# The eleventh gate and up tiles of a gated FFN as one seven-product block product, and two PSUM banks that change places

## The chip, the cores and the metric

The kernel runs on one core of a Trainium2 chip, in float32 throughout. The metric is the device time of one execution in microseconds; before the change its median over three runs is 2418.64 us (2414.57 to 2418.65). One more execution was taken with the hardware profiler; the profile, and every duration quoted here, is of that execution.

The engines are named as in the profile: PE is the matrix engine's matmuls and PEld its weight loads, DVE the vector engine, ACT the activation engine, POOL the GpSimd engine, and SP the engine whose queue issues nearly all transfers. A letter q behind an engine is its instruction queue (SPq).

## The reference, cut to what matters

The input x has 64 sequences of 128 tokens of 512 features. A normalised copy of x goes through a linear cross attention over a context, whose gated result is added to x; then the feed-forward part (FFN) works on a second normalised copy, here `x1n`:

```python
g = x1n @ gate_w.T * gate_s          # 512 -> 1408
u = x1n @ up_w.T   * up_s            # 512 -> 1408
hdn = silu(g) * u
out = x + tanh(g_ffn) * (hdn @ down_w.T * down_s)   # 1408 -> 512
```

The 1408 hidden units are eleven tiles of 128. The weights are given as inputs, so anything made from them is made once and used for all tokens.

## The kernel before, in words

**Groups.** The 64 sequences are worked in 16 groups of four, `g` from 0 to 15; a group is 512 tokens. Pass 1 (to about 430 us) normalises x and sums the scores over all sequences; between its groups the generator `prepare_weights` makes the weight combinations of the later pass. Pass 2 runs for each group the attention of group g interleaved with the FFN of group g - 1; the last FFN runs alone. `interleave` takes steps from the generators in proportion to given step counts (`FFN_STEPS` for the FFN), so that each `yield` in `ffn` is a place where attention work may be put. The program written so is then put in order, for each engine, by the framework's list scheduler, which may move an instruction ahead of others that don't depend on it. Each engine works its own list from front to back.

**Seven products in place of eight.** A product of two matrices, each seen as 2 by 2 blocks, needs eight block products if it is done plainly. `combine_a` makes four sums of one side's blocks (called GS1 to GS4 here) and `combine_b` four of the other's, and seven products of these, with a few additions of the results, give the same output. The kernel does this for tile pairs of gate and up: with the tiles j and 5 + j (`NJ` is 5) of both matrices, and for `x1nT` (features on partitions, 512 tokens) split into two halves of the features and two halves of the tokens (`HT`, 256 tokens). `combine_tokens` makes the four token sums `t` once for each group, on POOL.

In `ffn`, one j runs through the seven products GA11, GS1, GA12, GS2, GS3, GS4, GA22. Their results meet in PSUM: `bank_a` collects GA11 and GA12, `bank_f` holds GS1, and `bank_c` (one of the two halves of `banks_c`, which `next_c` gives in turn) starts from a copy of GA11 that ACT makes and collects GS2, GS3 and GA22; `bank_b` starts from a copy of `bank_c` after GS2 and collects GS4. GS1's result is copied to `m5` in SBUF. So between the products lie ACT copies, and DVE additions (`c22`, `c12`), and each of these must be done before the next product may write the bank that it read. `hidden` does silu on ACT and the multiplication on DVE. In these products the gate and the up tile of a j are two halves of one bank (`product`, two halves of 256 columns).

**The eleventh tile.** Eleven tiles make five pairs and one tile over (`REST` is 10). Its gate and up columns are worked plainly after the five j: `gu_rest[:, s]`, loaded in `constants`, against all of `x1nT`, four matmuls of 512 columns for gate into `bank_a` and four for up into `bank_f`; then one silu and one multiplication make `hrest`.

**Down.** The hidden result goes through seven products as well (`down_product`, DB11, DT1, DB21, DT2, DT3, DB22, DT4), five matmuls for each of two halves, with weights that `down` loads one product at a time; `down_rest` adds the eleventh tile's part, and `add` (DVE) adds the bank to x in SBUF. DB11 and DB21 use `bank_a`, DT1 and the first rest of the second pair `bank_f`, and the others `banks_c` and `bank_b`.

**The order of the transfers.** SP issues them in program order as the scheduler put them, each when its buffer is free: `gate_up(j + 1)` two transfers for each j, `down(m)` one for each product, between them the attention's.

A float32 matmul of the program is two matmul records on the chip, as the counts show: the eleventh tile's gate is 4 matmuls in each of 16 groups, and the profile has 128 records of it.

Of the kernel before, what the change touches and what calls it, by code (L numbers as in the profile page):

```python
# [8 lines left out]
F32 = mybir.dt.float32  # L9
AF = mybir.ActivationFunctionType  # L10
ALU = mybir.AluOpType
# [12 lines left out]
GA11, GS1, GA12, GS2, GS3, GS4, GA22 = range(7)  # L24
DB11, DB21, DB22, DT1, DT2, DT3, DT4 = range(7)
# [15 lines left out]
def flamingo_gated_layer(  # L41
# [21 lines left out]
    nc = tc.nc  # L63
    P = 128
# [3 lines left out]
    NC = DIM // P  # L68
    NI = INTER // P
    GB = 4  # L70
    NG = B // GB
    TOK = GB * S
    HT = TOK // 2
    HN = DIM // 2
    KC = NC // 2
    NJ = NI // 2
    REST = 2 * NJ
    assert S == P and H == NC and TOK == 512 and DIM == 512 and NI == REST + 1

    const = ctx.enter_context(tc.tile_pool(name="const", bufs=1))  # L80
# [36 lines left out]
    beta_sb = const.tile([P, NC], F32, name="beta_sb")  # L117
    gs_sb = const.tile([P, NI], F32, name="gs_sb")
    us_sb = const.tile([P, NI], F32, name="us_sb")
    gu_rest = const.tile([P, 2, NC, P], F32, name="gu_rest")  # L120
    dn_rest = const.tile([P, DIM], F32, name="dn_rest")


# [7 lines left out]
    bank_a = ps_bank.tile([P, TOK], F32, name="bank_a")  # L131
    bank_f = ps_bank.tile([P, TOK], F32, name="bank_f")
    bank_b = ps_bank.tile([P, TOK], F32, name="bank_b")
# [56 lines left out]
    def combine_a(engine, s, a11, a12, a21, a22):  # L190
        engine.tensor_tensor(s[0], a21, a22, ALU.add)  # L191
        engine.tensor_tensor(s[1], s[0], a11, ALU.subtract)
        engine.tensor_tensor(s[2], a11, a21, ALU.subtract)
        engine.tensor_tensor(s[3], a12, s[1], ALU.subtract)
# [40 lines left out]
    def constants():  # L235

        nc.sync.dma_start(out=gamma_sb, in_=gamma.rearrange("(c p) -> p c", p=P))
        nc.sync.dma_start(out=beta_sb, in_=beta.rearrange("(c p) -> p c", p=P))
        nc.sync.dma_start(out=gs_sb, in_=gate_s)
        nc.sync.dma_start(out=us_sb, in_=up_s)  # L240
        cols = slice(REST * P, INTER)
        for s, w in enumerate((gateT, upT)):
            nc.sync.dma_start(
                out=gu_rest[:, s], in_=w[:, cols].rearrange("(c p) i -> p c i", p=P)
            )

    def prepare_weights():

        constants()
        ds = once.tile([P, DIM], F32, name="ds")  # L250
        nc.sync.dma_start(out=ds, in_=down_s.partition_broadcast(P))
        nc.vector.tensor_scalar_mul(ds, ds, tanh_g[:, 1:2])
        yield


        raw = once.tile([P, NC, DIM], F32, tag="prep", name="wo_raw")
        nc.sync.dma_start(out=raw, in_=wo.rearrange("(c p) e -> p c e", p=P))
        nc.vector.tensor_scalar_mul(raw, raw, tanh_g[:, 0:1])
        t = once.tile([P, 4, KC, HN], F32, tag="prep2", name="wo_t")
        b = (  # L260
            raw[:, 0:KC, 0:HN], raw[:, 0:KC, HN:DIM], raw[:, KC:NC, 0:HN], raw[:, KC:NC, HN:DIM],
        )
        combine_b(nc.gpsimd, [t[:, i] for i in range(4)], *b)
        for m, src in ((DB11, b[0]), (DB21, b[2]), (DB22, b[3])):
            nc.sync.dma_start(out=wo_scr[m], in_=src)
        for i, m in enumerate((DT1, DT2, DT3, DT4)):
            nc.sync.dma_start(out=wo_scr[m], in_=t[:, i])
        yield


        for j in range(NJ + 1):
            i1, i2 = (j, NJ + j) if j < NJ else (REST, None)
            raw = once.tile([P, 2, DIM], F32, tag="prep", name="dn_raw")
            for q, i in enumerate((i1, i2)):
                if i is None:
                    nc.sync.dma_start(out=raw[:, q], in_=downT[i1 * P : (i1 + 1) * P])
                    nc.gpsimd.tensor_tensor(dn_rest, raw[:, q], ds, ALU.mult)
                    continue
                if j == NJ:
                    continue  # L280
                nc.sync.dma_start(out=raw[:, q], in_=downT[i * P : (i + 1) * P])
                nc.gpsimd.tensor_tensor(raw[:, q], raw[:, q], ds, ALU.mult)
            if j == NJ:
                yield
                continue
            t = once.tile([P, 4, HN], F32, tag="prep2", name="dn_t")
            b = (raw[:, 0, 0:HN], raw[:, 0, HN:DIM], raw[:, 1, 0:HN], raw[:, 1, HN:DIM])
            combine_b(nc.gpsimd, [t[:, i] for i in range(4)], *b)
            for m, src in ((DB11, b[0]), (DB21, b[2]), (DB22, b[3])):
                nc.sync.dma_start(out=dn_scr[m, :, j], in_=src)  # L290
            for i, m in enumerate((DT1, DT2, DT3, DT4)):
                nc.sync.dma_start(out=dn_scr[m, :, j], in_=t[:, i])
            yield

        for j in range(NJ):
            w = once.tile([P, 8, 2, KC, P], F32, tag="prep", name="gu_raw")
            i1 = slice(j * P, (j + 1) * P)
            i2 = slice((NJ + j) * P, (NJ + j + 1) * P)
            k1, k2 = slice(0, HN), slice(HN, DIM)
            for s, mat in enumerate((gateT, upT)):  # L300
                for m, k, i in ((GA11, k1, i1), (7, k1, i2), (GA22, k2, i2), (GA12, k2, i1)):
                    nc.sync.dma_start(
                        out=w[:, m, s], in_=mat[k, i].rearrange("(c p) i -> p c i", p=P)
                    )
            combine_a(
                nc.gpsimd, [w[:, m] for m in (GS1, GS2, GS3, GS4)],
                w[:, GA11], w[:, GA12], w[:, 7], w[:, GA22],
            )
            nc.sync.dma_start(out=gu_scr[0][j], in_=w[:, 0:3])
            nc.sync.dma_start(out=gu_scr[1][j], in_=w[:, 3:7])  # L310
            yield

    acc = banks_c[:, 1, :].rearrange("p (h s) -> p h s", h=H)

# [230 lines left out]
    def next_c():  # L545
        turn[0] ^= 1
        return banks_c[:, turn[0], :]
# [22 lines left out]
    def ffn(g, x_t, x1nT, tokens):  # L570
# [20 lines left out]
        for j in range(NJ):  # L591
# [34 lines left out]
                h11[:, j, :], h21[:, j, :], h12, h22[:, j, :],  # L626
            )
            yield
        for s, bank in enumerate((bank_a, bank_f)):
            for c in range(NC):  # L630
                nc.tensor.matmul(  # L631
                    bank, lhsT=gu_rest[:, s, c, :], rhs=x1nT[:, c, :],
                    start=(c == 0), stop=(c == NC - 1),
                )
            yield
        sil = work.tile([P, TOK], F32, tag="c", name="sil")
        nc.scalar.activation(sil, bank_a, AF.Silu, scale=gs_sb[:, REST:NI])
        nc.vector.scalar_tensor_tensor(
            hrest, bank_f, us_sb[:, REST:NI], sil, ALU.mult, ALU.mult
        )  # L640
        if g + 1 < NG:
            gu_next[0] = gate_up(0)

        def down_product(bank, m, lhs, start):
            dn = down(m)
            for i in range(2):
                for j in range(NJ):
                    nc.tensor.matmul(  # L648
                        bank[:, i * HN : (i + 1) * HN],
                        lhsT=lhs[:, j, i * P : (i + 1) * P],  # L650
                        rhs=dn[:, j, :],
                        start=(start and i == 0 and j == 0),
                        stop=(i == 1 and j == NJ - 1),
                        skip_group_check=True,
                    )
                yield

        def down_rest(bank, q, cols):
            for i in range(2):
                nc.tensor.matmul(  # L660
                    bank[:, i * HN : (i + 1) * HN],
                    lhsT=hrest[:, (2 * q + i) * P : (2 * q + i + 1) * P],
                    rhs=dn_rest[:, cols],
                    start=False, stop=(i == 1), skip_group_check=True,
                )

        def add(q, cols, bank):
            dst = x_t[q][:, :, cols]
            nc.vector.tensor_add(dst, dst, bank.rearrange("p (b d) -> p b d", b=2))

        d1, d2 = slice(0, HN), slice(HN, DIM)
        bank_c = next_c()
        yield from down_product(bank_a, DB11, h11, True)
        nc.scalar.copy(bank_c, bank_a)
        yield from down_product(bank_f, DT1, hs[:, 0], True)
        add(0, d2, bank_f)
        yield from down_product(bank_a, DB21, h21, False)
        down_rest(bank_a, 0, d1)
        add(0, d1, bank_a)
        yield  # L680
        yield from down_product(bank_c, DT2, hs[:, 1], False)
        nc.scalar.copy(bank_b, bank_c)  # L682
        down_rest(bank_f, 1, d2)
        add(1, d2, bank_f)
        yield
        yield from down_product(bank_c, DT3, hs[:, 2], False)
        add(1, d2, bank_c)
# [9 lines left out]
            nc.sync.dma_start(out=out[b : b + 2].rearrange("b s d -> s b d"), in_=x_t[q])  # L697

    gu_next = [gate_up(0)]
    FFN_STEPS = 1 + 7 * NJ + 2 + 17  # L700
    pending = (0, x_t, x1nT, combine_tokens(x1nT))
    x_next = load_x(1)
    c_next = [load_ctx(GB + j) for j in range(GB)]
# [71 lines left out]
```

## Time and profile before

| What | Value |
|---|---|
| median of three runs | 2418.64 us (2414.57 to 2418.65) |
| the profiled execution: its own time | 2416.87 us |
| its span, first to last instruction | 2415.1 us |
| PE busy | 2351.8 us, 97% of the span, 11480 matmul records |
| PEld busy | 1996.3 us, 83% |
| DVE, ACT, POOL busy | 802.0, 587.2, 686.2 us (33%, 24%, 28%) |
| the 16 DMA engines, mean busy share of the main queue | 49.1% |
| granted clock of the matrix engine, mean | 0.994 |
| one group of pass 2, from one start of the eleventh tile to the next (1384.4 to 1509.8 us) | 125.4 us |

How to read it: PE's busy time is the union of its records, so idle time is what is left. Of the 63 us in which PE did nothing, most lies before 507 us: the stretch from 0 to 507 us has PE busy 461.91 us. From there on a group of 125.40 us has PE busy 124.44 us. The waits of an engine are listed by the instruction that waited and the one that released it. The duration of a matmul record is longer than the distance to the next, since matmuls overlap; what counts is the distance from start to start.

### The profile page before, as it was taken

Reading aid. Unit: us, or ns where it says so; the run is one execution under the profiler, and the core shown is the slowest. Engines: PE = TensorE matmul, PEld = TensorE weight load, DVE = VectorE, ACT = ScalarE, POOL = GpSimd, SP = SyncE. Lnnn points to the kernel's source line nnn. Section 1 sums busy time; section 2 is a strip of 40 time slices with the busy share of each in tenths; the row PEclk is TensorE's granted clock in tenths of the full one; section 3 lists DMA queues with packets and bytes.
Section 4 is the critical chain, followed back from the end, with each engine's and each line's share of the span. In section 5 each row is a group of like instructions: output and inputs, shape, how many; then the busy total and the mean of one; then the engine's idle time right before and its main releaser. Section 6 shows DMA issues by size and latency. Waiting matters only on the chain.

```text
span 2415.1 us, 28827 instructions
## 1 busy us (share of the span) xinstructions
PE 2351.8 (97%) x11480; PEld 1996.3 (83%) x11480; DVE 802.0 (33%) x1541; ACT 587.2 (24%) x1076; POOL 686.2 (28%) x770
## 2 busy tenths in 40 slices
PE   7899998999999999999999999999999999999999
PEld 6777787888888888888888888888888888888887
DVE  6455433232323232323232323232323233232321
ACT  2232332312122222222221313131313131312121
POOL 3433003332323232323241414141414132232320
PEclk9999999999999999999999999999999999999999
DMA  7777544545454545444545444454545454544342
GB/s 262 243 251 251 172 144 131 214 131 185 139 173 150 176 143 173 146 166 148 168 157 165 164 146 162 159 168 140 175 145 165 140 178 133 182 133 149 118 147 72
DMA packets 136262, 396.31 MB, mean 164 GB/s; under 512 B 14272, under 2 KB 33856, under 8 KB 125248
## 3 DMA queue, kind: packets, MB, share of 16 engines
q1 hardware_dynamic: 132464, 392.63, 49.1%
q10 hardware_dynamic: 3664, 1.84, 0.3%
q8 instruction: 91, 1.49, 0.3%
q14 instruction: 43, 0.35, 0.0%
HBM read 345.26 MB, written 49.15 MB: 163 GB/s over the span
## 4 chain that ended last, share of the span: by engine, by line
PE 85%; DVE 5%; POOL 4%; DMA 3%; issue 1%; ACT 1%; SPq 0%; ACTq 0%; POOLq 0%; DVEq 0%
PE banks_c L169 17%; PE bank_a L169 12%; PE banks_c L648 9%; PE bank_b L169 6%; PE bank_a L648 6%; PE bank_f L169 4%; PE by L478 3%; PE bank_b L648 3%; PE bank_f L648 3%; PE pv L428 2%; PE bank_f L631 2%; PE bank_a L631 2%; PE bz L478 2%; PE bx L478 2%; PE banks_c L348 2%; PE po L438 2%
## 5 line engine op out<-in xcount | busy, mean ns | idle before, releaser
L169 PE MATMUL banks_c<-tcomb,gu 128*128 128x256 f32 x1920 | 453.9, 379 | 0.0
L169 PEld LDWEIGHTS banks_c<-tcomb,gu 128*128 128x128 f32 x1920 | 358.9, 190 | 46.3 <-ACT bank_b L604 0.7
L169 PE MATMUL bank_a<-x1nT,gu 128*128 128x256 f32 x1280 | 305.2, 381 | 6.8 <-ACT banks_c L596 6.7
L169 PEld LDWEIGHTS bank_a<-x1nT,gu 128*128 128x128 f32 x1280 | 237.6, 191 | 41.5 <-ACT banks_c L596 12.4
L146 POOL TENSOR_TENSOR rs<-ve,mhalf 128x1 f32<-128x1 f32 x128 | 72.5, 575 | 608.0 <-DVE ve L145 606.1
L191 POOL TENSOR_TENSOR hs<-h,h 128x256 f32<-128x256 f32 x80 | 58.0, 725 | 517.0 <-DVE h L584 517.0
L583 ACT ACTIVATE sil<-c,gs_sb 128x256 f32<-128x256 f32 x160 | 81.3, 508 | 345.1 <-DVE c L613 237.2
L169 PE MATMUL bank_b<-x1nT,gu 128*128 128x256 f32 x640 | 151.2, 379 | 0.0
L169 PE MATMUL bank_f<-tcomb,gu 128*128 128x256 f32 x640 | 151.2, 379 | 0.0
L613 DVE TENSOR_TENSOR c<-banks_c,m 128x512 f32<-128x512 f32 x80 | 55.3, 691 | 279.7 <-PE banks_c L169 279.7
L648 PE MATMUL banks_c<-dn_w,hs 128*128 128x256 f32 x640 | 146.0, 379 | 0.0
L648 PE MATMUL bank_a<-dn_w,h 128*128 128x256 f32 x640 | 143.5, 379 | 0.0
L648 PEld LDWEIGHTS bank_a<-dn_w,h 128*128 128x128 f32 x640 | 120.3, 190 | 16.3 <-issue 0.7
L169 PEld LDWEIGHTS bank_f<-tcomb,gu 128*128 128x128 f32 x640 | 120.5, 190 | 15.8
L169 PEld LDWEIGHTS bank_b<-x1nT,gu 128*128 128x128 f32 x640 | 120.5, 190 | 15.8
L648 PEld LDWEIGHTS banks_c<-dn_w,hs 128*128 128x128 f32 x640 | 119.2, 190 | 15.2 <-ACT bank_b L682 0.3
L596 ACT COPY banks_c<-bank_a 128x512 f32<-128x512 f32 x80 | 45.6, 570 | 301.6 <-PE bank_a L169 242.9
L584 DVE SCALAR_TENSOR_TENSOR h<-c,us_sb,sil 128x256 f32<-128x256 f32 x160 | 89.5, 559 | 83.8 <-ACT sil L583 83.8
L465 POOL TENSOR_TENSOR yT<-w_t,yT 128x512 f32<-128x512 f32 x64 | 81.1, 1268 | 121.3 <-ACT yT L460 121.3
L150 DVE BATCH_NORM_STATS2 st<-x_t 128x6 f32<-128x512 f32 x128 | 82.4, 683 | 82.2 <-DMA x_t<-in_x_dram 81.1
L584 DVE SCALAR_TENSOR_TENSOR h<-bank_a,us_sb,sil 128x256 f32<-128x256 f32 x80 | 38.6, 482 | 209.1 <-ACT sil L583 209.1
L188 POOL TENSOR_TENSOR tcomb<-x1nT 128x512 f32<-128x512 f32 x32 | 39.9, 1267 | 205.6 <-ACT x1nT L528 205.6
(134 smaller groups left out, 3651.9 us busy)
## 6 DMA issues: line engine op xcount, KB each, us to landing
gu<-gu_scr SPq DMA_DIRECT2D x80, 1024.0 KB, 4.9
dn_w<-dn_scr SPq DMA_DIRECT2D x112, 640.0 KB, 3.9
gu<-gu_scr SPq DMA_DIRECT2D x80, 768.0 KB, 4.3
x_t<-in_x_dram SPq DMA_DIRECT2D x64, 512.0 KB, 5.0
c_t<-in_ctxT_dram SPq DMA_DIRECT2D x128, 256.0 KB, 3.0
wo_w<-wo_scr SPq DMA_DIRECT2D x112, 256.0 KB, 2.8
w_scr<-w SPq DMA_DIRECT2D x32, 512.0 KB, 3.7
w_t<-w_scr SPq DMA_DIRECT2D x32, 512.0 KB, 3.6
```

The lines of the kernel that those rows point to most:

```text
L146: nc.gpsimd.tensor_tensor(dst, ve, mhalf[:, :n], ALU.pow)
L150: nc.vector.bn_stats(st, src)
L169: nc.tensor.matmul(bank[:, s * HT : (s + 1) * HT], lhsT=w[:, s, k, :], rhs=rhs[:, k, :], start=(start and s == 0 and k == 0), stop=(s == 1 ...
L191: engine.tensor_tensor(s[0], a21, a22, ALU.add)
L348: nc.tensor.matmul(acc[:, h, :], lhsT=c_t[j][:, h, :], rhs=qs[h][:, j * S : (j + 1) * S], start=(g == 0 and j == 0 and h == 0), stop=(g == ...
L465: nc.gpsimd.tensor_tensor(y, w[:, d], y, ALU.mult)
L478: nc.tensor.matmul(bank[:, i * HN : (i + 1) * HN], lhsT=lhs[:, k, i * P : (i + 1) * P], rhs=w[:, k, :], start=(start and i == 0 and k == 0 ...
L583: nc.scalar.activation(sil, src[:, 0:n], AF.Silu, scale=gs_sb[:, i : i + 1])
L584: nc.vector.scalar_tensor_tensor(dst, src[:, n : 2 * n], us_sb[:, i : i + 1], sil, ALU.mult, ALU.mult)
L613: nc.vector.tensor_add(c22, bank_c, m5)
L631: nc.tensor.matmul(bank, lhsT=gu_rest[:, s, c, :], rhs=x1nT[:, c, :], start=(c == 0), stop=(c == NC - 1),)
L648: nc.tensor.matmul(bank[:, i * HN : (i + 1) * HN], lhsT=lhs[:, j, i * P : (i + 1) * P], rhs=dn[:, j, :], start=(start and i == 0 and j == ...
```

## The change

The eleventh tiles of gate and up are treated as one more tile pair: gate's tile takes the place of the first tile (blocks a11, a12) and up's that of the second (a21, a22). `constants` loads the four blocks with four transfers in place of two; `gu_rest` doubles to eight blocks, and the new `rest_weights` makes the four sums on POOL, once, at the end of the step of `prepare_weights` that makes the eleventh tile's down weights.

In `ffn`, the seven products of the rest are each two matmuls of 256 columns (`rest_product`), in half a bank. Two halves of the tokens of gate come out in `bank_a` and in `bank_b` plus `m5`, those of up in `bank_c`, so there are two silus and two multiplications of 256 columns. A third bank half, `bank_d`, is taken with `next_c`, so that the down products' copy of DB11 can be made while the rest still uses `bank_c`. The first down product, DB11, stands in the middle of the seven, between GS2 and GS3, and it and DB21 use `bank_f`, where DT1 and the rest of the second pair now use `bank_a`. `gate_up(0)` of the next group is issued ahead of the eleventh tile, and no longer behind it. `FFN_STEPS` counts one step more.

```diff
-    gu_rest = const.tile([P, 2, NC, P], F32, name="gu_rest")
+    gu_rest = const.tile([P, 8, KC, P], F32, name="gu_rest")
...
-        for s, w in enumerate((gateT, upT)):
+        for m, mat, k in ((GA11, gateT, 0), (GA12, gateT, 1), (7, upT, 0), (GA22, upT, 1)):
             nc.sync.dma_start(
-                out=gu_rest[:, s], in_=w[:, cols].rearrange("(c p) i -> p c i", p=P)
+                out=gu_rest[:, m],
+                in_=mat[k * HN : (k + 1) * HN, cols].rearrange("(c p) i -> p c i", p=P),
             )
...
             if j == NJ:
+                rest_weights()
                 yield
...
+    def rest_weights():
+        combine_a(
+            nc.gpsimd, [gu_rest[:, m] for m in (GS1, GS2, GS3, GS4)],
+            gu_rest[:, GA11], gu_rest[:, GA12], gu_rest[:, 7], gu_rest[:, GA22],
+        )
...
-        for s, bank in enumerate((bank_a, bank_f)):
-            for c in range(NC):
-                nc.tensor.matmul(
-                    bank, lhsT=gu_rest[:, s, c, :], rhs=x1nT[:, c, :],
-                    start=(c == 0), stop=(c == NC - 1),
-                )
-            yield
-        sil = work.tile([P, TOK], F32, tag="c", name="sil")
-        nc.scalar.activation(sil, bank_a, AF.Silu, scale=gs_sb[:, REST:NI])
-        nc.vector.scalar_tensor_tensor(
-            hrest, bank_f, us_sb[:, REST:NI], sil, ALU.mult, ALU.mult
-        )
         if g + 1 < NG:
             gu_next[0] = gate_up(0)
...
+        def rest_product(bank, m, rhs, start):
+            for k in range(KC):
+                nc.tensor.matmul(
+                    bank[:, 0:HT], lhsT=gu_rest[:, m, k, :], rhs=rhs[:, k, :],
+                    start=(start and k == 0), stop=(k == KC - 1), skip_group_check=True,
+                )
+
+        def rest_silu(gate):
+            sil = work.tile([P, HT], F32, tag="sil", name="sil", bufs=3)
+            nc.scalar.activation(sil, gate, AF.Silu, scale=gs_sb[:, REST:NI])
+            return sil
+
+        def rest_hidden(tok, sil, up):
+            nc.vector.scalar_tensor_tensor(
+                hrest[:, tok], up, us_sb[:, REST:NI], sil, ALU.mult, ALU.mult
+            )
+
+        half = slice(0, HT)
+        bank_c = next_c()
+        m5 = work.tile([P, TOK], F32, tag="m5", name="m5")
+        rest_product(bank_a, GA11, b11, True)
+        nc.scalar.copy(bank_c[:, half], bank_a[:, half])
+        rest_product(bank_f, GS1, t[:, 0], True)
+        nc.scalar.copy(m5[:, half], bank_f[:, half])
+        yield
+        rest_product(bank_a, GA12, b21, False)
+        sil = rest_silu(bank_a[:, half])
+        rest_product(bank_c, GS2, t[:, 1], False)
+        nc.scalar.copy(bank_b[:, half], bank_c[:, half])
+        yield
+        bank_d = next_c()
+        yield from down_product(bank_f, DB11, h11, True)
+        nc.scalar.copy(bank_d, bank_f)
+        rest_product(bank_c, GS3, t[:, 2], False)
+        c22 = work.tile([P, TOK], F32, tag="c", name="c22")
+        nc.vector.tensor_add(c22[:, half], bank_c[:, half], m5[:, half])
+        rest_product(bank_b, GS4, b22, False)
+        c12 = work.tile([P, HT], F32, tag="h12", name="c12")
+        nc.vector.tensor_add(c12, bank_b[:, half], m5[:, half])
+        rest_product(bank_c, GA22, t[:, 3], False)
+        rest_hidden(slice(HT, TOK), rest_silu(c12), c22[:, half])
+        rest_hidden(half, sil, bank_c[:, half])
+        yield
...
-        bank_c = next_c()
-        yield from down_product(bank_a, DB11, h11, True)
-        nc.scalar.copy(bank_c, bank_a)
-        yield from down_product(bank_f, DT1, hs[:, 0], True)
-        add(0, d2, bank_f)
-        yield from down_product(bank_a, DB21, h21, False)
-        down_rest(bank_a, 0, d1)
-        add(0, d1, bank_a)
+        bank_c = bank_d
+        yield from down_product(bank_a, DT1, hs[:, 0], True)
+        add(0, d2, bank_a)
+        yield from down_product(bank_f, DB21, h21, False)
+        down_rest(bank_f, 0, d1)
+        add(0, d1, bank_f)
         yield
         yield from down_product(bank_c, DT2, hs[:, 1], False)
         nc.scalar.copy(bank_b, bank_c)
-        down_rest(bank_f, 1, d2)
-        add(1, d2, bank_f)
+        down_rest(bank_a, 1, d2)
+        add(1, d2, bank_a)
...
-    FFN_STEPS = 1 + 7 * NJ + 2 + 17
+    FFN_STEPS = 1 + 7 * NJ + 3 + 17
```

## The prediction

> **What bounds the kernel now.** I read the page's busy times first, then its 40 slices, then the busy times of one group, the waits of PE in that group, and at last the instructions in order of time around the eleventh tile.
>
> ```profile
> PE 2351.8 (97%) x11480; PEld 1996.3 (83%) x11480; DVE 802.0 (33%) x1541; ACT 587.2 (24%) x1076; POOL 686.2 (28%) x770
> ...
> PE   7899998999999999999999999999999999999999
> ...
> 0.00:507.00 507.00, 461.91 (x2369) 380.00 (x2370) 227.85 (x430) 154.12 (x260) 139.26 (x139) 0.97 0.63 206
> 1384.00:1509.40 125.40, 124.44 (x606) 106.74 (x605) 38.71 (x76) 29.15 (x55) 37.49 (x44) 1.00 0.48 159
> ```
>
> The window rows give start and end, length, and the busy time of PE, PEld, DVE, ACT and POOL. A group of pass 2 lasts 125.40 us and PE works 124.44 of them: PE bounds it, and all other engines have two thirds of it free. Before 507 us PE is idle for 45 us; transfers, POOL and DVE set the time there in places.
>
> The waits of PE in that group, then PE's instructions at the eleventh tile (start, length, engine, line):
>
> ```profile
> PE pt L455 <- DVE xn L162: 0.4, 1, 0.4
> PE bank_a L169 <- ACT banks_c L596: 0.4, 1, 0.4
> ```
>
> ```profile
> 1384.41 3.60 PE L631 MATMUL bank_a<-x1nT,gu_rest 128*128 128x512 f32 x8
> 1387.85 3.60 PE L631 MATMUL bank_f<-x1nT,gu_rest 128*128 128x512 f32 x8
> 1391.28 1.89 PE L478 MATMUL by<-wo_w,ys 128*128 128x256 f32 x8
> 1393.01 4.48 PE L648 MATMUL bank_a<-dn_w,h 128*128 128x256 f32 x20
> 1397.32 1.89 PE L478 MATMUL by<-wo_w,yT 128*128 128x256 f32 x8
> ```
>
> Starts, not lengths, give the price. Eight 512-column records take 1387.85 - 1384.41 = 3.44 us, 0.430 each; twenty of 256 columns take 1397.32 - 1393.01 = 4.31 us, 0.2155 each, and eight 1.73 us, 0.216. No wait stands between the rows, so what PE is spared here is time.
>
> [...] at 1478.04 us DVE's `xn` (L162) had waited 1.75 us for POOL, and the multiplication behind it, whose silu was done at 1477.19, began at 1478.77. It decides the prologue below. [...] The trace has 570 and 691 ns for n = 512[...]; silu and the multiplication at 256 columns have rows, 474 and 478 ns.
>
> **The change, part by part.**
>
> *Matmuls of the rest.* Gone per group: 16 records x 0.430 = 6.87 us (1384.41 to 1391.28). New: 7 products x 2 matmuls x 2 records = 28 x 0.2157 = 6.04 us. PE is spared 0.83 us a group, 12.4 us over the 15 groups with attention beside them.
>
> *New waits inside the block.* In the instruction order of the built kernel the fifteen groups read on PE: GA11, GS1, GA12, GS2, an attention product (`by`), DB11, another `by`, GS3, GS4, one matmul of DT1, GA22, the other nine of DT1. With 0.86 us for a product of the rest, and a consumer that starts 0.20 to 0.26 us after the next product starts (L637: 1388.11 against 1387.85):
> - GA12 waits for ACT's copy of GA11: ready at 0.86 + 0.26 + 0.36 + 0.05 = 1.53 us from the start, wanted at 1.73. An attention product (`bz`) now stands ahead of the block, so the silu and multiplication of j = 4, which ACT and DVE do first, are over by then.
> - DB11 overwrites `bank_f` 1.7 us after GS1's copy may begin; the copy takes 0.36. GS3 waits for the copies of `bank_b` and `bank_d`, done 0.9 us ahead or more.
> - GA22 waits for DVE's `c22`. DVE has ahead of it the addition of `by` and one statistics record: 11.42 + 0.72 + 0.60 + 0.42 + 0.05 = 13.2 us, wanted at 13.37.
>
> So nothing stalls, but slack is 0.2 us in two places. I take 0; the bounds are 0 and 0.3 us a group, 4.5 us.
>
> *Side work.* ACT: three copies and two silus, 2.02 us, for one silu of 0.69; DVE: two additions and two multiplications, 1.80 us, for one of 0.75. Some 1.3 and 1.1 us a group lie under 125 us of PE on engines busy 29 and 39 us; cost 0. Without that cover they would show as the stalls just bounded. `hrest` is ready at about 15.7 us and first wanted, after DT1 and DB21, beyond 22 us.
>
> *Moves.* `bank_a` and `bank_f` change places in down: each is free more than one product before its next write; 0. `gate_up(0)` passes SP's place by one block: its buffer is freed at j = 3 either way, the transfer (4.3 to 4.9 us) has no reader before the next group; 0. DB21's weights wait for DB11's buffer, and now have GS3 to GA22 and DT1 to arrive, over 8 us for 3.9; 0. One more step in `FFN_STEPS` shifts `pv`, `po`, `bx` and `bz` by one product. The places of both 0.4 us waits (the transposes behind `po` and the copy behind them) read the same as before. I take 0; the bounds are both waits gone (-12 us in all) and one more such wait a group (+6).
>
> *The last group* has no attention for cover. There the order is GS1, one matmul of DB11, GA12: DB11 overwrites `bank_f` at once, and waits 0.26 + 0.36 + 0.05 = 0.67 us for the copy of GS1. Of the 0.83 us, 0.15 remain.
>
> *Prologue.* Loads: four of 128 KB for two of 256. Sums: four POOL operations at 0.73 us (L191 to L194 at this shape), 2.9 us once. Their length matters less than their place: in the built order three of them stand ahead of the `rstd` of the third group, and the first waits for up's loads. Before, in order of time:
>
> ```profile
> 32.14 0.47 SPq L243 DMA_DIRECT2D gu_rest<-in_upT_dram  x1
> ...
> 36.58 1.01 POOL L146 TENSOR_TENSOR rstd<-ve,mhalf 128x4 f32<-128x4 f32 x1 [6.53 <-DVE ve L145]
> ...
> 37.62 1.00 DVE L162 TENSOR_SCALAR xn<-x_t,mean_var,rstd 128x512 f32<-128x512 f32 x2 [0.53 <-POOL rstd L146]
> ...
> 42.33 0.68 DVE L379 TENSOR_TENSOR w<-banks_c,m5p 128x512 f32<-128x512 f32 x1
> ```
>
> Up's load landed after 5.5 us, at 37.6. Then three sums, 2.2 us, and `rstd` 1.0: `rstd` is ready at 40.8, not 37.6. DVE's queue stands behind `xn`, and in it the addition at L379 that PE waited for already (0.26 us, to 43.06). Of the 3.2 us, waits of 0.2 and 0.1 us for data are absorbed; I take +2.9 us. PE releases the context buffers that SP waits for later, so I let it last. With the shortest landing (3.6 us) it is 1.2 us, and later transfer waits could swallow it all. The loads also shift SP's order through pass 1, where single waits last 4 to 10 us; a gain or a loss of 5 us is in reach, and no row bounds it better.
>
> **The sum**, on the profiled execution's own time: 2416.87 - 12.4 - 0.15 + 2.9 = 2407.2 us (span 2405.4). The median stands 1.8 us above that execution, so I state 2409.0.
>
> **The rivals.**
> - *Pass 1 costs more* (and the 0.2 us slacks fail): 8 to 13 us lost in the prologue in place of 2.9, or 5 there and 0.3 us a group, give 2414 to 2419, no change. For it: 45 us of idle PE, and a chain there full of transfers. Against: the sums take 2.9 us, and only one `rstd` is late.
> - *Pass 1 costs nothing, or an old wait goes*: 2398 to 2406. For it: the next wait for a transfer (5 us, at 83.6 us) may swallow the delay. Against: PE frees the buffer that this transfer waits for.
> - *Slower, by one wait*: `c22` stands in DVE's queue behind the whole normalisation that follows `by`, not behind one statistics record. In the trace that chain (1399.97 to 1403.36, with POOL's `rs` in it) takes 3.4 us: GA22, and with it DT1, would wait about 2.6 us a group, 39 us, giving 2436. It decides from 1.15 us a group (0.83, and 4.8 us over 15 groups). Against: the built order has `c22` after the first statistics record.
> - *The change does not do what it says*: the block would not be cheaper if 256-column records cost more than 0.245 us. Against: they take 0.216 here.
>
> **How the numbers follow.** A measurement of this kernel can tell about 0.2% from no change, 4.8 us: faster is below 2413.8, slower above 2423.5. The sum as worked out, within the small bounds, has 0.65 (2404 to 2414, its own range); the cheaper pass 1 or a vanished wait 0.12; the dearer pass 1 or failing slack 0.16; the slower wait 0.07. The first two are faster: 0.77; the third is the same: 0.16; the last 0.07. The range, 2400 to 2417, leaves out somewhat under 2 in 10: the ends of the cheap and of the dear case, and the last.
>
> **What would show it.** In the profile after: 448 records (28 in each of 16 groups) read `gu_rest` at 256 columns, and none at 512; a group lasts 124.6 us; PE's waits in it are still two of 0.4 us, and none at GA12, GS3 or GA22 of the rest; the third group's `rstd` starts near 39.8 us and PE stands about 3 us at 43. A group of 125.4 us or more, with a PE wait released by DVE's `c22` or ACT's copy, would prove the slack wrong; a group of 124.6 with an unchanged total would prove the prologue.

## The result, and the profile after

The changed kernel takes **2404.50 us** (median of 4 runs, 2401.93 to 2405.83) beside 2416.61 us for the kernel before (4 runs): ratio 0.9951, 95% interval [0.9933, 0.9968]. The same instructions were measured three times more, in other sets of runs: 0.9952 [0.9940, 0.9965], 0.9956 [0.9944, 0.9969] and 0.9960 [0.9948, 0.9972]. The four ratios average 0.9955, which is 10.9 us of 2416. The prediction said 2409.0, in a range of 2400 to 2417, faster by more than 0.2%. Its profiled execution took 2405.83 us, span 2404.0.

The lines of the page after that answer to those of before, the busy times and PE's 40 slices:

```profile
PE 2339.4 (97%) x11672; PEld 2033.2 (85%) x11672; DVE 802.7 (33%) x1589; ACT 609.7 (25%) x1140; POOL 689.1 (29%) x774
...
PE   7898999999999999999999999999999999999999
```

The window rows of the kernel after (start and end, length, and busy time of PE, PEld, DVE, ACT and POOL):

```profile
0.00:507.00 507.00, 461.63 (x2366) 380.28 (x2367) 228.90 (x428) 154.62 (x261) 143.11 (x142) 0.97 0.62 205
1380.02:1504.59 124.57, 123.61 (x618) 109.00 (x617) 38.48 (x79) 30.57 (x59) 37.35 (x44) 1.00 0.48 160
```

PE has 192 instructions more (448 narrow for 256 wide) and is busy 12.4 us less. A group of pass 2 lasts 124.57 us, and PE still works all but 0.96 us of it, as before. POOL is busy 2.9 us longer, the four sums. The waits of PE in that group are the same two:

```profile
PE pt L464 <- DVE xn L162: 0.4, 1, 0.4
PE bank_a L169 <- ACT banks_c L605: 0.4, 1, 0.4
```

Measured over 14 groups, from the first block's start to the fifteenth's, a group took (2262.06 - 506.75) / 14 = 125.379 us before and (2251.57 - 507.49) / 14 = 124.577 after: 0.802 us less. PE's instructions at the block, by start, length and name:

```profile
1379.67 1.03 PE L658 MATMUL bank_a<-x1nT,gu_rest 128*128 128x256 f32 x4
1380.53 1.03 PE L658 MATMUL bank_f<-tcomb,gu_rest 128*128 128x256 f32 x4
1381.39 1.03 PE L658 MATMUL bank_a<-x1nT,gu_rest 128*128 128x256 f32 x4
1382.26 1.03 PE L658 MATMUL banks_c<-tcomb,gu_rest 128*128 128x256 f32 x4
...
1390.89 1.03 PE L658 MATMUL banks_c<-tcomb,gu_rest 128*128 128x256 f32 x4
1391.75 1.03 PE L658 MATMUL bank_b<-x1nT,gu_rest 128*128 128x256 f32 x4
1392.62 0.59 PE L645 MATMUL bank_a<-dn_w,hs 128*128 128x256 f32 x2
1393.05 1.03 PE L658 MATMUL banks_c<-tcomb,gu_rest 128*128 128x256 f32 x4
```

The starts lie 0.86 us apart, four records of 0.216: nothing waits. The third row is GA12, which needs ACT's copy of GA11 (L677, 1380.73 to 1381.09); it has 0.30 us to spare. The last is GA22, which needs `c22`. On DVE, at the same place:

```profile
1391.09 0.69 DVE L498 TENSOR_TENSOR x_t<-x_t,by 128x512 f32<-128x512 f32 x1 [5.36 <-PE by L487]
1391.81 0.69 DVE L150 BATCH_NORM_STATS2 st<-x_t 128x6 f32<-128x512 f32 x1
1392.42 0.41 DVE L691 TENSOR_TENSOR c<-banks_c,m 128x256 f32<-128x256 f32 x1
```

`c22` ends at 1392.83, and GA22 starts at 1393.05. In pass 1 the wait that was predicted is there. The timeline of all engines, cut to the chain: `rstd`'s input `ve` on DVE, three sums on POOL, of which the first waited for up's load, `rstd` behind them, DVE's addition, and PE, which stood still for 3.25 us:

```profile
33.86 0.15 DVE L145 TENSOR_SCALAR ve<-mean_var 128x4 f32<-128x4 f32 x1
...
34.81 0.73 POOL L193 TENSOR_TENSOR gu_rest<-gu_rest 128x256 f32<-128x256 f32 x1 [7.25 <-DMA gu_rest<-in_upT_dram]
35.49 0.72 POOL L191 TENSOR_TENSOR gu_rest<-gu_rest 128x256 f32<-128x256 f32 x1
36.30 0.72 POOL L192 TENSOR_TENSOR gu_rest<-gu_rest 128x256 f32<-128x256 f32 x1
36.98 1.02 POOL L146 TENSOR_TENSOR rstd<-ve,mhalf 128x4 f32<-128x4 f32 x1
...
42.85 0.67 DVE L388 TENSOR_TENSOR w<-banks_c,m5p 128x512 f32<-128x512 f32 x1
43.57 1.92 PE L357 MATMUL banks_c<-q,c_t 128*128 128x128 f32 x8 [3.25 <-DVE w L388]
```

### The profile page after: what moved, and what is told of

Read it like the earlier page. It is cut to its first block, busy times and chain, and to the rows that moved or that the text cites. A ratio compares the mean times of both kernels' runs of the same rounds, so it can differ in the third digit from the quotient of the medians.

```text
span 2404.0 us, 29313 instructions
## 1 busy us (share of the span) xinstructions
PE 2339.4 (97%) x11672; PEld 2033.2 (85%) x11672; DVE 802.7 (33%) x1589; ACT 609.7 (25%) x1140; POOL 689.1 (29%) x774
## 4 chain that ended last, share of the span: by engine, by line
PE 84%; DVE 5%; DMA 4%; POOL 4%; issue 1%; ACT 1%; SPq 0%; ACTq 0%; POOLq 0%; DVEq 0%
PE banks_c L169 17%; PE bank_a L169 12%; PE banks_c L645 9%; PE bank_b L169 6%; PE bank_f L645 6%; PE bank_f L169 4%; PE by L487 3%; PE bank_a L645 3%; PE bank_b L645 3%; PE pv L437 2%; DMA x_t<-in_x_dram 2%; PE bz L487 2%; PE bx L487 2%; PE banks_c L357 2%; PE po L447 2%; PE banks_c L658 2%
## 5 line engine op out<-in xcount | busy, mean ns | idle before, releaser
L169 PEld LDWEIGHTS bank_a<-x1nT,gu 128*128 128x128 f32 x1280 | 238.2, 190 | 42.1 <-ACT banks_c L605 12.4
L645 PE MATMUL bank_f<-dn_w,h 128*128 128x256 f32 x640 | 143.7, 379 | 0.5 <-ACT m L679 0.5
L645 PEld LDWEIGHTS bank_f<-dn_w,h 128*128 128x128 f32 x640 | 120.3, 190 | 16.6 <-ACT m L679 0.9
L593 DVE SCALAR_TENSOR_TENSOR h<-c,us_sb,sil 128x256 f32<-128x256 f32 x160 | 79.8, 499 | 83.7 <-ACT sil L592 83.7
```

The lines of the kernel that those rows point to most:

```text
L169: nc.tensor.matmul(bank[:, s * HT : (s + 1) * HT], lhsT=w[:, s, k, :], rhs=rhs[:, k, :], start=(start and s == 0 and k == 0), stop=(s == 1 ...
L593: nc.vector.scalar_tensor_tensor(dst, src[:, n : 2 * n], us_sb[:, i : i + 1], sil, ALU.mult, ALU.mult)
L645: nc.tensor.matmul(bank[:, i * HN : (i + 1) * HN], lhsT=lhs[:, j, i * P : (i + 1) * P], rhs=dn[:, j, :], start=(start and i == 0 and j == ...
```

## The experiments

Three sets of runs, each with its own runs of the kernel before (medians 2415.02, 2415.59 and 2414.52 us). "Against the changed kernel" means its run in the same set, where there is one.

### Are narrow matmuls no loss by themselves?

The kernel before, its sixteen records for the eleventh tiles cut into thirty-two of 256 columns:

```diff
-            for c in range(NC):
-                nc.tensor.matmul(
-                    bank, lhsT=gu_rest[:, s, c, :], rhs=x1nT[:, c, :],
...
+            for tok in (slice(0, HT), slice(HT, TOK)):
+                for c in range(NC):
+                    nc.tensor.matmul(
+                        bank[:, tok], lhsT=gu_rest[:, s, c, :], rhs=x1nT[:, c, tok],
...
```

> The kernel before with the eleventh tile done plainly in matmuls of 256 columns, 16 in place of 8, in the same two banks; nothing else differs. Theory A (the gain is the eighth product, and width costs next to nothing): 32 records x 0.2157 = 6.90 us where before has 6.87, a group of 125.4 us, the same time as before within 1 us. Rival C (the gain comes from narrow records, which let the weight loads hide or let attention in sooner): a group shorter by 0.3 us or more, 5 us or more below before. Rival D (narrow records are dearer, and the change won against that): a group longer by 0.3 us or more.

Measured: 2414.39 us, ratio 0.9997 [0.9989, 1.0006]; a group takes 125.416 us, 0.037 more than before, 2.3 ns for each of the 16 records more. So what the change gains is the four records of thirty-two that it leaves out (28 in place of 32), not their width.

### The banks, and the place of DB11

The kernel before with the two banks of down changed and nothing else:

```diff
-        yield from down_product(bank_a, DB11, h11, True)
-        nc.scalar.copy(bank_c, bank_a)
-        yield from down_product(bank_f, DT1, hs[:, 0], True)
...
+        yield from down_product(bank_f, DB11, h11, True)
+        nc.scalar.copy(bank_c, bank_f)
+        yield from down_product(bank_a, DT1, hs[:, 0], True)
...
```

> The kernel before, with nothing of the change but the two banks of down that change places (DB11 and DB21 in bank_f, DT1 in bank_a). My step Moves: no difference, group 125.4 us, within 1 us of the kernel before. Rival: DB11 in bank_f waits for the reader of up's 512 columns that the kernel before has just put there (the multiplication at L637), about 0.9 us a group at most where no attention product stands between: 5 to 13 us slower.

Measured: 2415.20 us, ratio 0.9997 [0.9988, 1.0005]; a group takes 125.383 us. Only in the last group, without attention, does PE have a new wait, 0.96 us for the weights of DB21. The changed kernel with DB11 behind all seven products, not between the fourth and the fifth:

```diff
-        bank_d = next_c()
-        yield from down_product(bank_f, DB11, h11, True)
-        nc.scalar.copy(bank_d, bank_f)
         rest_product(bank_c, GS3, t[:, 2], False)
...
         rest_hidden(half, sil, bank_c[:, half])
+        bank_d = next_c()
+        yield from down_product(bank_f, DB11, h11, True)
+        nc.scalar.copy(bank_d, bank_f)
```

> The changed kernel with DB11 behind all seven products of the eleventh tile, not between GS2 and GS3. In the 15 groups an attention product still stands between GS2 and GS3; GS3, GS4, GA22 follow at once. Theory A (the copies and additions are so short that an attention product or one product of 0.86 us covers each): GA22 waits at most 0.3 us for c22, a group is 124.6 to 124.9 us, the time 0 to 5 us above the changed kernel. Rival E (DB11 in the middle is what keeps PE from waiting): 0.67 us or more a group in waits of PE for ACT or DVE, 10 us above the changed kernel, which eats most of the gain.

Measured: 2404.58 us, ratio 0.9956 [0.9943, 0.9970]; a group takes 124.569 us, beside 124.577 in the changed kernel. Neither edit is worth anything by itself: an attention product stands where DB11 stood, and covers the copies as well.

### What the slack is worth

First the order of the two DVE additions was turned round in the source:

```diff
-        nc.vector.tensor_add(c22[:, half], bank_c[:, half], m5[:, half])
         rest_product(bank_b, GS4, b22, False)
         c12 = work.tile([P, HT], F32, tag="h12", name="c12")
         nc.vector.tensor_add(c12, bank_b[:, half], m5[:, half])
+        nc.vector.tensor_add(c22[:, half], bank_c[:, half], m5[:, half])
```

> The changed kernel, with one pair of DVE instructions in the other order: c22 is added after c12, not before. PE's order is the same. My slack reckoning: c12 can start 0.2 us after GS4's end, and takes 0.41; one short statistics record and c22 follow, 0.5; GA22 then waits 0.6 to 0.8 us a group, in which the group takes 125.2 to 125.4 us: 9 to 12 us slower than the changed kernel, level with the kernel before. Rival H (the wait is absorbed later in the group, by the two waits of 0.4 us or by a wait for a transfer): PE shows the wait but the group lasts 124.6 to 124.8, less than 3 us slower. Rival J (the slack is wider than reckoned): no wait at GA22, no difference.

Measured: 2405.15 us, ratio 0.9956 [0.9944, 0.9969], and no wait at GA22. The edit did not do what it says: the scheduler puts the two additions back, and DVE's records stand in the changed kernel's order. The run tells nothing of the slack and counts as one more measurement of the changed kernel.

The order was then forced, by letting `c22` reuse the buffer that ACT's silu of `c12` has to read first:

```diff
-        nc.vector.tensor_add(c22[:, half], bank_c[:, half], m5[:, half])
         rest_product(bank_b, GS4, b22, False)
-        c12 = work.tile([P, HT], F32, tag="h12", name="c12")
-        nc.vector.tensor_add(c12, bank_b[:, half], m5[:, half])
+        nc.vector.tensor_add(c22[:, half], bank_b[:, half], m5[:, half])
+        sil2 = rest_silu(c22[:, half])
+        nc.vector.tensor_add(c22[:, half], bank_c[:, half], m5[:, half])
```

> The changed kernel with the rival's wait brought about: c12 is first added into the buffer of c22, so that c22 can be added only once ACT's silu has read c12; on DVE it then stands behind the first half of the normalisation that follows by. On PE four more matmuls of DT1 go ahead of GA22, 1.72 us. By the changed kernel's own durations c22 is done some 2.9 us after GS4's end (c12 0.2 + 0.4, statistics and rs 1.3, xn 0.5, c22 0.4) and GA22 is wanted 2.15 us after it: a wait of 0.7 us a group, bounds 0.3 and 1.2. The rival as I priced it (a PE wait in the block shows in full in the group): group 125.0 to 125.8 us, total 5 to 15 us over the changed kernel, about 10. Rival H (waits are absorbed): PE waits at GA22 show, the group stays at 124.6, total within 2 us.

Measured: 2414.22 us, ratio 0.9998 [0.9990, 1.0006], 8.3 us over the changed kernel of its set and level with the kernel before. The waits of PE after 500 us have one row more than the changed kernel's, and at one block DVE and PE read (two views of the timeline, DVE's first):

```profile
PE banks_c L658 <- DVE c L694: 5.4, 15, 0.4
```

```profile
1397.55 0.55 DVE L162 TENSOR_SCALAR xn<-x_t,mv,rs 128x512 f32<-128x512 f32 x1 [0.60 <-POOL rs L146]
1398.01 0.42 DVE L694 TENSOR_TENSOR c<-banks_c,m 128x256 f32<-128x256 f32 x1
...
1395.80 2.32 PE L645 MATMUL bank_a<-dn_w,hs 128*128 128x256 f32 x10
1398.48 1.13 PE L658 MATMUL banks_c<-tcomb,gu_rest 128*128 128x256 f32 x4 [0.36 <-DVE c L694]
1399.45 2.32 PE L645 MATMUL bank_a<-dn_w,hs 128*128 128x256 f32 x10
```

The rival of the prediction, `c22` behind a normalisation with POOL's `rs` in it, is real where the order brings it about. A group takes (2259.15 - 506.30) / 14 = 125.204 us, 0.63 more. The wait as printed is 0.36. By starts the rest is found: ten records of 0.2157 from 1395.80 end at 1397.96, so GA22 came 0.52 late, and its own four took 0.97 in place of 0.86. 0.52 + 0.11 = 0.63: the whole of it reached the group, none was absorbed. It would have been more if the scheduler had not put four more matmuls of DT1 in front: without them GA22 would have been wanted at 1396.23, and `c22` came at 1398.43, 2.2 us later.

### The prologue

Loads and sums alone, in the kernel before, with its sixteen plain matmuls:

```diff
-        for s, w in enumerate((gateT, upT)):
+        for m, mat, k in ((GA11, gateT, 0), (GA12, gateT, 1), (7, upT, 0), (GA22, upT, 1)):
...
+                combine_a(
+                    nc.gpsimd, [gu_rest[:, m] for m in (GS1, GS2, GS3, GS4)],
+                    gu_rest[:, GA11], gu_rest[:, GA12], gu_rest[:, 7], gu_rest[:, GA22],
+                )
```

> The kernel before with the change's four loads and four POOL sums only; the eleventh tile stays eight plain matmuls of 512 columns on the loaded blocks, and the sums are not used. Theory A (the late rstd of the third group holds PE up for some 3 us at 43 us, and later waits of pass 1 swallow the delay): a PE wait of about 3 us at L379 near 43 us where before has 0.26, but the time within 1.5 us of before, 2415 to 2418; a group of pass 2 stays at 125.38 us. Theory B (the delay lasts, as the prediction took it): 2419 to 2420, about 3 us above before. If the order of the loads makes pass 1 longer by itself: 5 us or more above.

Measured: 2417.31 us, ratio 1.0011 [1.0003, 1.0019]: 2.6 us dearer, 0.7 to 4.6, with a PE wait of 2.71 us at 43.11 us. The interval lies above zero, but its lower end is within the 1.5 us of Theory A: the delay most likely lasts, and this run does not part the loads from the sums.

The changed kernel with the four loads ahead of the small constants:

```diff
-        nc.sync.dma_start(out=gamma_sb, in_=gamma.rearrange("(c p) -> p c", p=P))
...
         for m, mat, k in ((GA11, gateT, 0), (GA12, gateT, 1), (7, upT, 0), (GA22, upT, 1)):
...
+        nc.sync.dma_start(out=gamma_sb, in_=gamma.rearrange("(c p) -> p c", p=P))
...
```

> The changed kernel with the four loads of the eleventh tile issued as the first of the constants, ahead of the small ones, so that the sums on POOL have their data before the third group's rstd is due. Theory A: the PE wait near 43 us is back to under 0.5 us (3.25 in the changed kernel), the time no more than 1.5 us below the changed kernel. Theory B: 3 us below the changed kernel, about 2401.5. Both: a group of pass 2 stays at 124.58 us.

Measured: 2405.02 us, ratio 0.9959 [0.9947, 0.9972]; a miss, since PE still waited 2.30 us at 44.90. The sums were over by 33.0 us, ahead of `rstd`, which now followed its input `ve` at once. But `ve` itself came late. Four of DVE's lines in this run, and below the dots, for comparison, the first two of them in the run with the sums held back, which is described further on:

```profile
29.48 0.94 DVE L162 TENSOR_SCALAR xn<-x_t,mean_var,rstd 128x512 f32<-128x512 f32 x1 [0.92 <-POOL rstd L146]
30.34 1.21 DVE L188 TENSOR_TENSOR t<-xnT,t 128x512 f32<-128x512 f32 x1
37.50 0.14 DVE L145 TENSOR_SCALAR ve<-mean_var 128x4 f32<-128x4 f32 x1
40.67 0.49 DVE L253 TENSOR_SCALAR ds<-ds,tanh_g 128x512 f32<-128x512 f32 x1 [0.89 <-DMA ds<-in_down_s_dram]
...
27.85 0.55 DVE L162 TENSOR_SCALAR xn<-x_t,mean_var,rstd 128x512 f32<-128x512 f32 x1 [0.92 <-POOL rstd L146]
28.31 0.68 DVE L188 TENSOR_TENSOR t<-xnT,t 128x512 f32<-128x512 f32 x1
```

Beside the sums on POOL, from 29.4 to 33.0 us, DVE's instructions lasted longer. From the second group's `rstd` to the third's `ve` DVE took 9.45 us (28.05 to 37.50); with the sums held back 7.70 (26.42 to 34.12). Then it waited 0.89 us for the load of `ds`, which was issued 1.3 us later than in the changed kernel, counted from that `rstd`. (By the clock the whole execution lay 1.9 us behind the changed kernel's before any moved load was issued, at 22.0 us: the first sum of `wgc` started at 13.99 us, there at 12.11.) So the sums are not free ahead of `rstd` either, and the order of the loads on SP has its own price.

Loads and sums three weight tiles later:

```diff
-        cols = slice(REST * P, INTER)
-        for m, mat, k in ((GA11, gateT, 0), (GA12, gateT, 1), (7, upT, 0), (GA22, upT, 1)):
...
         for j in range(NJ):
...
+            if j == NJ - 1:
+                rest_weights()
...
     def rest_weights():
+        cols = slice(REST * P, INTER)
+        for m, mat, k in ((GA11, gateT, 0), (GA12, gateT, 1), (7, upT, 0), (GA22, upT, 1)):
...
```

> The changed kernel, with the four loads of the eleventh tiles and their four sums made three weight tiles later, so that no sum stands ahead of the third group's rstd on POOL. PE's order is the same. Theory B (the delay lasts): PE's 3.25 us wait at 43 us is gone or back at 0.3, the second project stage to the third takes 22 us in place of 26, and the time is 2 to 3 us under the changed kernel's. Theory A (swallowed): the wait at 43 us is gone and the time is the changed kernel's within 1 us. Theory G (the loads only push the transfers behind them, whatever stands on POOL): the wait moves to a later place in pass 1, and the time is the changed kernel's.

> The changed kernel as it is, timed against the kernel before in as many rounds as the others. Theory B (the delay that loads and sums bring to pass 1 lasts to the end, 2 to 3 us): 9 to 10 us faster, 14 groups x 0.80 us = 11.2, 0.6 at the end, less 2.6. Theory A (the delay is swallowed by a later wait for a transfer): 11.8 us faster. Theory F (something in pass 1 is also cheaper by chance of the transfers): 13 us faster or more.

Measured: 2400.42 us, ratio 0.9940 [0.9927, 0.9954], beside the changed kernel's 2402.36, 0.9952 [0.9940, 0.9965]. The wait at 43 us fell from 3.19 us to 0.21. The source moved them to the last step of the weights, and the scheduler to the point behind the first tile of down; in pass 1 the orders of DVE and of SP's transfers changed in many places too, and a few of PE's matmuls, which the expectation did not foresee. 1.9 us is about the predicted size, but the intervals overlap. The changed kernel of this set came out 11.6 us under the kernel before by the ratio, 13.2 by the medians, and not the 9 to 10 of Theory B: by itself that speaks for a swallowed delay, though the interval, 8.5 to 14.5, holds all three theories. A cleaner version leaves every load and every PE, DVE and SP instruction where it is, and holds back the four sums alone:

```diff
+            if j == 0:
+                for m in (GS1, GS3):
+                    nc.gpsimd.tensor_tensor(
+                        gu_rest[:, m, 0, 0:4], raw[:, 0, 0:4], raw[:, 1, 0:4], ALU.add
+                    )
```

> The changed kernel with one thing moved: two tiny POOL additions, written over later, make the four sums of the eleventh tiles wait until the first tile of down has been scaled. The orders of PE, DVE and SP are those of the changed kernel; on POOL the four sums now stand behind the rstd of the third and fourth groups. Theory B (the late rstd costs time to the end): the wait of some 3 us at 43 us goes, 0.3 at most is left, the second to the third project stage takes 22 us in place of 25 to 28, and the time is 2 to 3 us under the changed kernel's. Theory A (swallowed later): the wait goes, the time is the same within 1 us. Theory G (it is the loads, in SP's queue, that delay pass 1): the wait at 43 us stays at 1 us or more.

> The changed kernel as it is, as the control of this set: 10 to 13 us under the kernel before, as in the earlier sets; a PE wait of 3 us at 43 us.

> The changed kernel with loads and sums three weight tiles later, as run before in another set (15 us under the kernel before, where the changed kernel was 13 us under). Theory B: again 2 to 3 us under the changed kernel of this set, no wait at 43 us. Theory A: the same within 1 us, and the earlier difference was chance.

Measured in one set: the sums gated 2402.90 us, 0.9945 [0.9933, 0.9958]; the changed kernel 2405.88, 0.9960 [0.9948, 0.9972]; loads and sums later 2399.24, 0.9932 [0.9920, 0.9944]. The control's 9.7 us by the ratio (8.6 by the medians) is a little under the 10 to 13 expected. With the sums gated the timeline of pass 1 reads:

```profile
34.12 0.15 DVE L145 TENSOR_SCALAR ve<-mean_var 128x4 f32<-128x4 f32 x1
...
34.35 1.01 POOL L146 TENSOR_TENSOR rstd<-ve,mhalf 128x4 f32<-128x4 f32 x1 [6.54 <-DVE ve L145]
...
40.05 0.67 DVE L393 TENSOR_TENSOR w<-banks_c,m5p 128x512 f32<-128x512 f32 x1
...
40.78 1.16 PE L362 MATMUL banks_c<-q,c_t 128*128 128x128 f32 x8 [0.20 <-DVE w L393]
```

`rstd` starts 0.23 us behind `ve`, where the kernel after took 3.12 us (33.86 to 36.98): 2.89 us earlier. PE waits 0.20 us where it waited 3.25 (3.28 in the control). From one GS1 of `project` to the next (what the expectation calls the second and third stage) it took 22.49 us beside 26.37 in the control; before the change, 22.07. The medians differ by 3.0 us, as expected. The chain from the sums to `rstd` to PE's wait is shown, since PE, DVE and SP have the same order in both. That it costs 2 to 3 us of the total is less certain: the two intervals overlap here, and the other evidence is the 2.6 us (0.7 to 4.6) of loads and sums together. The version with the loads moved as well is 6.6 us under the changed kernel, with an interval apart from it. In both of its profiles the wait of 4 to 6 us for DVE's `w` near 90 us, which the changed kernel and the gated one have, and the kernel before as well (3.87 us at 89.35), is gone too; smaller ones stand at 64 us (1.8) and, in one, at 110 (3.05). What took it away is not shown: the loads moved, and with them the order of DVE and of the other transfers. The version has the lowest medians of all, 15 us under the kernel before in both sets and 2 to 7 under the changed one, but its interval overlaps that of the gated one.

## Why the prediction was right

- *Matmuls of the rest.* Right. 28 records take 6.04 us (3.45 from GA11 to the next `by`, 1.73 for GS3 and GS4, 0.86 for GA22), as worked out, and the group gained 0.802 of the 0.83. Where the other 0.03 us went no view shows. The narrow version of the old matmuls, 0.037 us a group dearer, says that the count made the difference.
- *New waits inside the block.* Right, and as tight as said: 0.30 us at GA12, 0.22 at GA22, against 0.2 and 0.17 worked out. The difference is small errors in durations. The 0.36 us of ACT's copy and the 0.42 of DVE's addition, both of 256 columns, no row of the kernel before showed (its 570 and 691 ns are those of 512 columns); in the kernel after the three copies average 358, 374 and 357 ns and the two additions 407. In the forced version the slack is spent, and the gain with it.
- *Side work* and *Moves.* Right at 0: ACT and DVE took it beside PE (by the mean lengths in the kernel after, 2.07 us a group on ACT and 1.78 on DVE), the two waits of 0.4 us stayed, the banks alone changed nothing but the last group. The earlier `gate_up(0)` and the added step were not run alone; the spared records account for what the group gained, so little room is left for them.
- *The last group.* PE waited for the copy of GS1 as predicted (by starts 2360.54 - 2359.91 = 0.63 us for the 0.67). From the fifteenth block to the end it gained 153.04 - 152.43 = 0.61 us, where one full group and this one were to give 0.98. Two small costs were in no term: the records from 2360.54 and from 2367.57 us took 0.11 us more than their number asks (0.54 for two, 0.97 for four).
- *Prologue.* Right in mechanism, and right in size in the end: three sums stood ahead of `rstd` and made it 2.89 us late, for the 3.2 worked out, and PE's wait was 3.25 us for the 3 named. POOL kept the order of its list there: it stood idle until up's load was in at 34.81 us, though `ve` was done at 34.01, and `rstd` ran behind the sums. The clock time of it was wrong: `rstd` started at 36.98 us, not near 39.8, since up's load landed at 34.8 and this whole prologue ran earlier (its first GS1 of `project` at 26.43 us, where the execution before had 28.70). Loads and sums alone cost 2.6 us, and holding the sums back gave 3.0. That both lie so near the 2.9 is in part luck. The prediction has the wait alone reach the end, whole. In the run of loads and sums alone the delay grew behind the wait (9.37 us to the next GS1 in place of 7.71, at a granted clock of 0.79 from 40 to 48 us; last section), and later waits took a part up: counted from the first GS1 of `project` (26.67 us, before the change 28.70), it was 3.75 us at the fourth GS1 (100.87 and 99.15) and 2.5 at the first block of the eleventh tile (507.24 and 506.75).
- *The sum.* 9.65 us was predicted on the execution's own time. The pieces measured give 14 x 0.802 + 0.61 - 2.6 = 9.2; the four comparisons give 10.9 on average, the first 12.1, the last 8.6. The interval of the 2.6 alone, 0.7 to 4.6, covers the difference. One candidate was the clock described below: in all four profiles with plain matmuls a stretch near 425 us, about the first attention, ran slow (a granted clock of 0.50 or 0.51 in a window of 4 us), and with the change only in three of ten (0.50, 0.50 and 0.57). The executions without a profile do not bear it out: the mean granted clock is 0.9938 over 61 of the kernel before and 0.9936 over 19 of the changed one.
- *The rivals.* The cheaper and the dearer pass 1 didn't come about; the wait for `c22` did only where it was forced, and then cost 9 us (15 x 0.63), not 39: the scheduler covers part of it with other matmuls, which the prediction did not count on. Records of 256 columns cost what they did before, 0.216 us.

## What to carry to other kernels

When PE is the bound, count its records by their starts: here that gave 0.83 us a group (6.87 - 6.04), and 0.802 came; then look at each value the new order makes PE wait for, and at what stands ahead of its producer in that engine's queue, because 0.2 us of slack a group is all that kept this gain. The one-time preparation was priced here not by its own length but by what was queued behind it: 2.9 us of POOL work held PE up for 3 us because it waited for a load in front of an `rstd`; behind the `rstd` it did not, and further ahead of it, without the wait, DVE took 9.45 us in place of 7.70 beside it. And look at the order that was built: one of these edits was silently undone, another moved more than was meant.

## What the runs showed of the hardware

PE's wait near 43 us cost more than its length in seven of the eight runs where it was 2.3 us or longer, and in them the granted clock was below 1.00 there (0.50 to 0.87, from 40 or from 44 us to 48). A row of the windows of the kernel after (the third column from the end is the granted clock):

```profile
44.00:48.00 4.00, 4.00 (x21) 3.92 (x21) 3.56 (x6) 1.06 (x1) 4.00 (x3) 0.60 0.35 102
```

The same row of another run of the same instructions, the one whose additions had been put back:

```profile
44.00:48.00 4.00, 4.00 (x26) 3.67 (x25) 4.00 (x7) 1.65 (x2) 4.00 (x4) 1.00 0.54 154
```

After a wait of 3.25 us the clock was 0.60 from 44 to 48 us, and the eight matmuls behind the wait (L357) took 1.92 us; after one of 3.09 us, in the other run, it stayed at 1.00 and they took 1.16. The price can be read from the end of the wait to the next GS1 of `project`, the same work in every run. It was 7.71 or 7.72 us in the six runs where PE waited there for less than 1 us (the kernel before among them). Of the eight where it waited 2.3 to 4.0 us, one took 7.72 as well, five took 9.15 to 9.37, and two 10.56 and 10.58: 1.4 to 2.9 us on top of the wait in seven of eight.

The length of the wait alone did not decide it: after 3.09 us the next GS1 came after 7.72 us, and in the run with the loads first, where PE waited 2.30, after 9.36. In the kernel before, the longest waits near 420 us are 1.82 us (to 409.10) and 1.90 us (to 419.97), and in the three windows of 4 us from 420 us on the clock was 0.66, 0.50 and 0.56. What decides whether the clock falls no run shows.

Part of the scatter between executions of the same kernel, 2411.4 to 2421.4 us in the 61 of the kernel before, goes with the clock: the fourteen with a mean granted clock of 0.992 or less average 2416.8 us, the ten with 0.996 average 2413.3.

Some instructions of DVE and POOL lasted longer where they ran at once. With a sum beside it on POOL, a pair of `xn` on DVE took 1.40 us in the changed kernel (38.03 us), and 1.00 with the sums held back (35.39); with the loads first, single ones of DVE's took 0.94 and 1.21 us in place of 0.55 and 0.68, and two of the sums 0.90 and 1.06 in place of 0.73.
